# Layer 1 row loads moved behind other weights, and GpSimd's part of the stage reordered, in a two-layer graph kernel

## The chip, the cores and the metric

The kernel runs on one core of a Trainium2 chip. A core has TensorE for matrix products, VectorE and ScalarE for elementwise work, GpSimd (POOL in the profile) for elementwise work and for issuing transfers, and SyncE (SP), which only issues transfers. Sixteen DMA engines serve all queues. Times are device microseconds of the core, from separate executions; one more execution was taken under the profiler. The number to predict is the median time of the changed kernel.

## The reference, cut to what matters

Both layers work on 128 graphs of 64 nodes with 768 features, all in float32. Layer 0 is an attention whose weights come from the features themselves, with three linear maps (left, self, right). Layer 1 has twelve heads with maps q, k and v. Each is followed by a residual and a layer norm.

```python
x, adj: (128, 64, 768), (128, 64, 64)
# layer 0
u = softmax(h @ h.T / sqrt(768)) * adj;  attn = u / (sum(u) + 1e-10)
ctx = upper(attn) @ (h @ Wl.T + bl) + diag(attn) * (h @ Ws.T + bs) + lower(attn) @ (h @ Wr.T + br)
x = layernorm(x + relu(layernorm(ctx) * gamma + beta))
# layer 1
q, k, v = x @ Wq + bq, x @ Wk + bk, x @ Wv + bv        # 12 heads of 64
s = q @ k.T / 8 + beta * adj, masked to -9e15 where adj <= 0
x = layernorm(x + softmax(s) @ v)
```

## The kernel before, in words

The tokens are cut into 16 blocks of 512 (8 graphs). A block's tokens are four tiles `o` of 128 tokens by 768 features, and also a transposed form, with features on partitions, that feeds the products: `hT` for layer 0, `xT` for layer 1.

Products are done with fewer multiplications than the plain form, from sums of quarters (or sixths) of both factors. Weights in such summed forms lie ready in DRAM (`lr_d` for left and right together, `d_s` for self, `v_d`, `qk_d`) and are loaded anew for each block on SyncE's queue into rings of buffers: `wlr`, `ws`, `wv`, `wqk`. Sums of the token side are made by GpSimd: `combined` (L403) makes the operands of a layer 0 block and `second_level` (L467) their second sums `q`; `combined4` (L417, recorded as L420) makes the last operand, number 3; `fifteen` (L422) makes those of layer 1.

The loop over `n` (L1202) is a software pipeline: layer 1 of block `n` runs among layer 0 of block `m = n + 1` and the ends of block `p = n - 1`. Its stages for TensorE are, in order:

- left and right of block `m` together (`both_sides`, L761, matmuls L784), from `m = 3` on: seven products, each of seven inner ones, 49 steps in all. Nine `wlr` weights of the next product are loaded when the present one begins. The products come in the order 7, 1, 2, 6, 5, 4, 3. These 13 blocks are called deep here.
- self of block `m` (`self_part`, matmuls L520): seven products in two halves, 14 places, three `ws` weights each.
- `values` of block `n` (wv, L459), with the attention products of block `m` (L832) among them.
- `projected` of block `n`, twice (wqk, L459), for q and k.

The order of everything else is written out by hand with `at(hooks, place, f)`. `left` and `right` have 14 places each over the 49 steps; place `k` of both together comes ahead of step `49 k / 28`, with `right` counted from 14. `own` has 14 places in the self stage, `val` 15 in values, `qk[0]` and `qk[1]` 15 each. Short pieces are put into queues (`later`) and taken one by one in `step` after each product step. Every engine runs its instructions in the order in which they were recorded, so what stands in front in a queue holds up what stands behind.

The lines that the change touches:

- The output of layer 0, `o` of block `n`, is stored to DRAM as rows (`x1d`, L888, `stored`) by GpSimd and read back in another order (`sq`, L387, function `squares`) by SyncE: four loads of 384 KB, each into 32 partitions. VectorE turns `sq` into `xT` by six transposes (L396, `turned`). GpSimd's `fifteen` then makes the layer 1 sums. The buffer `sq` is a single one; after the sixth transpose ScalarE's queue loads the input rows of the next block into it, and VectorE makes `hT` from them in values.
- In a deep block the four loads stand at `right` 5 to 8, which is among the last steps of products 5 and 4; nine `wlr` of product 3 are recorded among them.
- `combined4` and the four stores stand at `left` 6; so they come between additions `o` (L1070) of the block before, which wait for VectorE's shares of attention (L1067).
- `out_dram` (L1107) is the output of the block before, four stores of 384 KB by GpSimd, which follow the norm by ScalarE (L1103) near the end of the left and right stage.

A transfer reports its landing on one of eight semaphores of the queue, taken in turn; SyncE waits, before it issues a transfer, until the transfer that had the same semaphore eight issues earlier has landed.

Of the kernel before, what the change touches and what calls it, by code (L numbers as in the profile page):

```python
# [17 lines left out]
P = 128  # L18
# [5 lines left out]
T = 4  # L24
# [28 lines left out]
DEEP = 3  # L53
# [16 lines left out]
def gnn_two_layers(ctx: ExitStack, tc, x, adj, wl, bl, ws, bs, wr, br, gamma, beta,  # L70
                   wq, bq, wk, bk, wv, bv, abeta, out):
    nc = tc.nc
# [51 lines left out]
    for half, sign in ((0, 1), (1, -1)):  # L124
        for g in range(2):
            nc.gpsimd.affine_select(
                out=side[half * L : (half + 1) * L, g, :], in_=side[half * L : (half + 1) * L, g, :],
# [4 lines left out]
    blocks = {}  # L132
# [44 lines left out]
    def freed():  # L177

        while first:
            first.popleft()[1]()  # L180
# [236 lines left out]
    def combined4(S, n=None):  # L417

        S[3] = sums[:, KC : KC + HC]
        last_sum[n] = nc.gpsimd.tensor_tensor(S[3], S[2], S[6], ALU.subtract)  # L420
# [391 lines left out]
    def context0(n):  # L812


        blk = blocks[n]
        o, dg = blk["x"], blk["dg"]
        by_act = n > 0
        if by_act:
            total, nm, var, std, rstd = (st.tile([P, T], F32, tag=f"c{k}", name=f"c{k}") for k in range(5))

        def unused():
            return l1s_p.tile([P, T * 6 * L], F32, tag="s", name="unused")[:, 0:D]

        banks = {}

        def multiplied(ts):
            freed()
            for t in ts:
                for h in range(2):
                    ps = banks[t, h] = ps_mm.tile([P, 512], F32, tag="mm", name="ps_ctx")  # L830
                    for g in range(2):
                        nc.tensor.matmul(ps[g * L : (g + 1) * L, 0:HALF], lhsT=blk["aT"][:, t, g * L : (g + 1) * L],  # L832
                                         rhs=blk["lr"][t][:, g, h * HALF : (h + 1) * HALF], start=True, stop=True)

        def part(t):
            if t % 2 == 0:
                multiplied((t, t + 1))
            for h in range(2):
                cols = slice(h * HALF, (h + 1) * HALF)
                nc.vector.scalar_tensor_tensor(o[t][:, cols], o[t][:, cols], dg[:, t : t + 1],  # L840
                                               banks.pop((t, h))[:, 0:HALF], ALU.mult, ALU.add)
            if by_act:
                nc.scalar.activation(unused(), o[t], AF.Identity, accum_out=total[:, t : t + 1])  # L843
            elif t == T - 1:
                rest(moments(key, o, 1e-12))

        key = ("o", n)

        def squares():
            nc.vector.tensor_scalar(nm, total, -1.0 / D, None, ALU.mult)  # L850
            for t in range(T):
                nc.scalar.activation(unused(), o[t], AF.Square, bias=nm[:, t : t + 1], accum_out=var[:, t : t + 1])

        def roots():
            nc.vector.tensor_scalar(std, var, 1.0 / D, 1e-12, ALU.mult, ALU.add)
            nc.scalar.activation(std, std, AF.Sqrt)

        def inverse():
            nc.vector.reciprocal(rstd, std)
            rest([(nm[:, t : t + 1], rstd[:, t : t + 1]) for t in range(T)])  # L860

        def affine(t, mean, rstd):
            nc.vector.scalar_tensor_tensor(o[t], o[t], mean, affine_of["gamma"], ALU.add if by_act else ALU.subtract,
                                           ALU.mult)

        def affine2(t, mean, rstd):
            nc.vector.scalar_tensor_tensor(o[t], o[t], rstd, affine_of["beta"], ALU.mult, ALU.add)

        def residual(t):
            nc.vector.scalar_tensor_tensor(o[t], o[t], 0.0, blk["xa"][t], ALU.max, ALU.add)  # L870

        squared = 0 < n < NBLK - 1
        blk["x_d"] = x_d = tc.dram_tile([NTOK, D], F32, name=f"x1d_{n}") if squared else None

        def lowered(mrs):
            for t, (mean, rstd) in enumerate(mrs):
                nc.vector.scalar_tensor_tensor(nm[:, t : t + 1], mean, -1.0, rstd, ALU.mult, ALU.mult)

        def norm(t, mean, rstd):
            if by_act and (n < NBLK - 1 or t % 2 == 0):  # L880
                nc.scalar.activation(o[t], o[t], AF.Identity, bias=nm[:, t : t + 1], scale=rstd)
            else:
                nc.vector.tensor_scalar(o[t], o[t], mean, rstd, ALU.subtract, ALU.mult)

        def stored():
            settle(key)
            for t in range(T):
                nc.gpsimd.dma_start(out=x_d[t * P : (t + 1) * P, :], in_=o[t])  # L888

        blk["stored"] = stored  # L890

        def rest(factors):
            for t, mr in enumerate(factors):
                fs = partial(affine, t, *mr), partial(affine2, t, *mr), partial(residual, t)
                later(key, *(fs if by_act else (fs[0], lambda fs=fs: (fs[1](), fs[2]()))))
            mrs = moments(key, o, 1e-5)
            fs = [partial(norm, t, *mr) for t, mr in enumerate(mrs)]
            later(key, *((tiny(partial(lowered, mrs)), *(f if n == NBLK - 1 and t % 2 else act(f) for t, f in enumerate(fs))) if by_act else
                         (lambda: (fs[0](), fs[1]()), lambda: (fs[2](), fs[3]()))))

        return [partial(part, t) for t in range(T)], (squares, roots, inverse)
# [300 lines left out]
    for n in range(NBLK):  # L1202
        m, p = n + 1, n - 1
        left, right, own, val = {}, {}, {}, {}
        qk = [{}, {}]

        def at(hooks, place, f, *args):
            hooks.setdefault(place, []).append(partial(f, *args))
# [24 lines left out]
        if not last:  # L1233
            if n > 0:
                if m + 1 < NBLK:
                    at(left, 4, edges, m + 1)
                at(*((left, 11) if m < DEEP else (right, 13)), sides, m)
                sq1 = {}

                def begin1():  # L1240
                    blocks[n]["sq1"], sq1["fs"] = squares(blocks[n]["x_d"], nc.sync)


                when, place = right, 5 if m >= DEEP else 10
                at(when, place, begin1)
                fetch = {}

                def begin2():
                    fetch["fs"] = loads(m)

                at(val, 3, begin2)
                for t in range(T):
                    at(val, 3 + t, lambda t=t: fetch["fs"][t]())
                for a in range(P // Q):
                    at(when, place + a, lambda a=a: sq1["fs"][a]())
                at(own, 0, settle, ("f", p))

                def turn1():
                    blocks[n]["xT"] = turned(("t1", n), blocks[n]["sq1"], f"xT_{n}")
                    later(("m", n), *mask(n), queue=urgent)  # L1260

                at(own, 3, turn1)

                def sums1():
                    settle(("t1", n))
                    blocks[n]["S"] = fifteen(blocks[n]["xT"], False)

                at(own, 11, sums1)
                at(val, 0, lambda: fifteenth(blocks[n]["S"]))
                at(left, 6, lambda: combined4(blocks[m]["S"]))  # L1270
                if n > 1:
                    for k in range(T):
                        at(left, 1 + k, begun, ("o", n), T - 1 - k)
                at(*((left, 6) if n > 1 else (right, 1)), blocks[n]["stored"])
                if m + 1 < NBLK:
                    sq = {}

                    def begin():
                        blocks[m + 1]["sq"], sq["fs"] = squares(x_b[m + 1])

                    at(own, 11, begin)
                    for a in range(P // Q):
                        at(own if a < 3 else val, 11 + a if a < 3 else 0, lambda a=a: sq["fs"][a]())
                if m == DEEP:
                    settle("d")
                if m < DEEP:
                    side_part(m, "l", None, left)
                    side_part(m, "r", None, right)
                    at(own, 0, lambda: nc.vector.tensor_tensor(bias_lr[:, :, HALF:D], bias_lr[:, :, HALF:D],
                                                               bias_lr[:, :, 0:HALF], ALU.subtract))  # L1290
                else:
                    for t, f in enumerate(both_sides(m, {**left, **{2 * len(ORDER) + k: f for k, f in right.items()}})):
                        at(own, 1 + t, f)
                self_part(m, None, own)
# [33 lines left out]
    n = NBLK - 1  # L1328
# [127 lines left out]
```

## Time and profile before

| what | us |
|---|---|
| median of 3 runs (lowest, highest) | 2916.44 (2909.95, 2923.62) |
| profiled execution | 2916.36 |
| its span, first to last instruction | 2914.3 |
| TensorE busy | 2807.8 |
| VectorE busy | 1950.4 |
| ScalarE busy | 1101.7 |
| GpSimd busy | 945.0 |
| granted TensorE clock, mean of the span | 0.991 |

A row of the timeline has start and length in microseconds, the engine (PE is TensorE, DVE VectorE, ACT ScalarE, POOL GpSimd, SPq SyncE's queue), the line, the operation, what it writes and reads, and in brackets how long the engine stood idle before it and what ended that. A row of the window view has busy time and count for each of PE, weight loads, DVE, ACT and POOL, then the granted clock, the share of the DMA engines' time in use, and GB/s. Clock and shares are fractions of one.

### The profile page before, as it was taken

To read this page: it belongs to the slowest core of one execution; us is meant where nothing else is said; L and a number is where in the kernel's file an instruction comes from. 1 tells how busy PE (TensorE), PEld (TensorE's weight loads), DVE (VectorE), ACT (ScalarE), POOL (GpSimd) and SP (SyncE) were. 2 spreads that over 40 slices of the span, in tenths; PEclk is the share of its full clock that TensorE was granted. 3 is DMA by queue.
4 is the path that set the end of the run, shared out by engine and by line. 5 is a ranking of instruction groups with operands and counts; after the bars stand their busy time and mean duration, and the time that the engine had idled before them with its cause. 6 is when DMAs were issued, how large, how long until landed. Compare 5 with 4: busy or idle time off the path is not lost.

```text
span 2914.3 us, 49295 instructions
## 1 busy us (share of the span) xinstructions
PE 2807.8 (96%) x17962; PEld 2019.9 (69%) x17962; DVE 1950.4 (67%) x3399; ACT 1101.7 (38%) x1907; POOL 945.0 (32%) x1231
## 2 busy tenths in 40 slices
PE   9999999999999999999998999999999999999997
PEld 5558677585776858668585775857758577685786
DVE  6787777575675766667676675766757567575655
ACT  0003324344343442535334343443434424344254
POOL 3234233514134151522615125141341414315121
PEclk9999999999999999999999999999999999999998
DMA  8788695948669486684957759586594866848542
GB/s 316 217 278 267 187 289 179 263 132 256 190 191 255 135 269 177 209 234 144 276 153 225 216 155 275 135 268 189 186 246 126 264 187 196 250 135 254 166 123 91
DMA packets 398493, 604.85 MB, mean 208 GB/s; under 512 B 49296, under 2 KB 282256, under 8 KB 398256
## 3 DMA queue, kind: packets, MB, share of 16 engines
q1 hardware_dynamic: 349520, 506.73, 59.3%
q0 software_dynamic: 17456, 72.96, 6.6%
q10 hardware_dynamic: 31280, 22.03, 3.7%
q8 instruction: 145, 2.38, 0.3%
q14 instruction: 92, 0.75, 0.1%
HBM read 530.00 MB, written 78.45 MB: 209 GB/s over the span
## 4 chain that ended last, share of the span: by engine, by line
PE 85%; DMA 7%; DVE 4%; issue 2%; POOL 1%; SPq 1%; ACT 1%; DVEq 0%; POOLq 0%; ACTq 0%
PE ps_X L459 25%; PE ps_Y L459 17%; PE ps_X L520 10%; PE ps_Y L784 10%; PE ps_X L784 8%; PE ps_Y L520 7%; DMA wlr<-lr_d 4%; PE ps_ctx L832 3%; PE sc L996 2%; PE u L663 2%; PE ps_y L1059 2%; DMA h_q<-in_L_gnn_Wq_dram 0%; POOL o L1070 0%; ACT eT L1029 0%; DMA h_v<-in_L_gnn_Wv_dram 0%
## 5 line engine op out<-in xcount | busy, mean ns | idle before, releaser
L408 POOL TENSOR_TENSOR sums<-hT 128x768 f32<-128x768 f32 x16 | 28.9, 1808 | 851.9 <-PE ps_X L459 841.2
L1029 ACT ACTIVATE eT<-s 32x384 f32<-32x384 f32 x512 | 266.6, 521 | 31.9 <-DVE s L1012 25.5
L1070 POOL TENSOR_TENSOR o<-o,share 128x192 f32<-128x192 f32 x240 | 134.7, 593 | 410.8 <-DVE share L1067 391.5
L574 DVE TENSOR_TENSOR lr<-ps_Y,u_deep 128x384 f32<-128x384 f32 x273 | 151.6, 555 | 140.2 <-PE ps_Y L784 123.9
L459 PE MATMUL ps_X<-xT,wqk 128*128 128x256 f32 x1024 | 236.0, 381 | 3.0 <-DMA wqk<-qk_d 2.0
L843 ACT ACTIVATE unused<-o 128x768 f32<-128x768 f32 x60 | 50.6, 843 | 476.4 <-DMA sq<-in_x_dram 227.5
L459 PEld LDWEIGHTS ps_X<-xT,wqk 128*128 128x128 f32 x1024 | 195.5, 191 | 30.7 <-DVE w_deep L362 2.4
L784 PE MATMUL ps_Y<-wlr,q 128*128 128x384 f32 x546 | 208.6, 491 | 0.0
L972 ACT ACTIVATE qk<-ps_X,bq 128x256 f32<-128x256 f32 x128 | 60.6, 473 | 388.8 <-PE ps_X L459 388.5
L975 DVE TENSOR_TENSOR qk<-qk,ps_X 128x512 f32<-128x512 f32 x160 | 109.8, 686 | 137.1 <-PE ps_X L459 74.7
L520 PE MATMUL ps_X<-ws,hT 128*128 128x384 f32 x540 | 179.8, 487 | 3.0 <-DVE u L551 3.0
L459 PE MATMUL ps_Y<-more,wqk 128*128 128x256 f32 x768 | 181.4, 379 | 0.0
L459 PE MATMUL ps_X<-sums,wqk 128*128 128x256 f32 x768 | 180.3, 381 | 0.5 <-issue 0.5
L784 PE MATMUL ps_X<-wlr,q 128*128 128x384 f32 x364 | 151.3, 497 | 19.5 <-issue 17.6
L459 PEld LDWEIGHTS ps_Y<-more,wqk 128*128 128x128 f32 x768 | 145.9, 190 | 19.8
L459 PEld LDWEIGHTS ps_X<-sums,wqk 128*128 128x128 f32 x768 | 144.6, 190 | 20.9 <-issue 0.9
L520 PEld LDWEIGHTS ps_X<-ws,hT 128*128 128x128 f32 x540 | 102.2, 190 | 74.8 <-DVE u L551 3.9
L975 DVE TENSOR_TENSOR qk<-qk,ps_Y 128x512 f32<-128x512 f32 x160 | 108.2, 677 | 67.7 <-PE ps_Y L459 65.1
L574 DVE TENSOR_TENSOR u_deep<-ps_X,lr 128x384 f32<-128x384 f32 x195 | 107.7, 553 | 66.7 <-PE ps_X L784 61.3
L784 PEld LDWEIGHTS ps_Y<-wlr,q 128*128 128x128 f32 x546 | 101.5, 190 | 67.3
L437 POOL TENSOR_TENSOR more<-xT 128x512 f32<-128x512 f32 x32 | 43.1, 1347 | 281.3 <-DVE xT L396 173.4
L784 PE MATMUL ps_X<-wlr,sums 128*128 128x384 f32 x234 | 93.7, 510 | 38.6 <-DMA wlr<-lr_d 35.8
(269 smaller groups left out, 6258.1 us busy)
## 6 DMA issues: line engine op xcount, KB each, us to landing
wlr<-lr_d SPq DMA_DIRECT2D x819, 192.0 KB, 4.1
wqk<-qk_d SPq DMA_DIRECT2D x480, 256.0 KB, 2.6
wv<-v_d SPq DMA_DIRECT2D x240, 256.0 KB, 6.2
ws<-d_s SPq DMA_DIRECT2D x180, 192.0 KB, 4.4
ws<-in_L_gnn_W_self_dram SPq DMA_DIRECT2D x135, 192.0 KB, 6.3
xa<-in_x_dram SPq DMA_DIRECT2D x64, 384.0 KB, 5.8
out_dram<-o POOLq DMA_DIRECT2D x60, 384.0 KB, 6.5
sq<-in_x_dram ACTq DMA_DIRECT2D x56, 384.0 KB, 10.8
```

The lines of the kernel that those rows point to most:

```text
L459: nc.tensor.matmul(ps[:, h, :], lhsT=a, rhs=b, start=start and h == 0 and k == 0, stop=k == len(fs[h]) - 1, skip_group_check=True)
L520: nc.tensor.matmul(ps, lhsT=a, rhs=b, start=(c == 0 and i in (1, 2, 5)), stop=(c == len(fs) - 1), skip_group_check=True)
L574: nc.vector.tensor_tensor(dst, view(ps), add, ALU.add)
L663: nc.tensor.matmul(u[g * L : (g + 1) * L, t, :], lhsT=xT[:, c, tok], rhs=xT[:, c, tok], start=(c == 0), stop=(c == KC - 1))
L784: nc.tensor.matmul(ps, lhsT=a, rhs=b, start=(k == 0 and j in (1, 2, 5)), stop=(k == len(fs) - 1), skip_group_check=True)
L832: nc.tensor.matmul(ps[g * L : (g + 1) * L, 0:HALF], lhsT=blk["aT"][:, t, g * L : (g + 1) * L], rhs=blk["lr"][t][:, g, h * HALF : (h + 1) * ...
L972: nc.scalar.activation(dst[:, h], ps[:, h, :], AF.Identity, bias=bias["qk"[h]][:, c : c + 1], scale=float(sign))
L975: nc.vector.tensor_tensor(dst, dst, ps, ALU.add if sign > 0 else ALU.subtract)
L996: nc.tensor.matmul(sc[t // 2, r][g * L : (g + 1) * L, t % 2, c, :], lhsT=q[rows, c, tok], rhs=k[rows, c, tok], start=True, stop=True)
L1029: nc.scalar.activation(e[to[0], :, to[1]], pairs[rows, :, cols], AF.Exp, scale=1.0 / SCALE)
L1059: nc.tensor.matmul(y[h, r][cols, t, c, :], lhsT=eT[rows, 2 * h + t, c, cols], rhs=by_parity[rows, 2 * h + t, 2 * c + m, g, :], start=True, ...
L1070: nc.gpsimd.tensor_tensor(res, res, share[:, t], ALU.add)
```

## The change

The four loads of layer 1 rows move from `right` 5 to 8 to `right` 12 and 13 and `own` 0 and 1 (before block 3 they stood at `right` 10 to 13). As SyncE's queue stands in a deep block, the first three now come behind the nine `wlr` of the last product and ahead of the first three `ws`, and the fourth behind these three. The transposes of `xT` begin at `own` 4, not `own` 3, and the mask's three VectorE instructions, queued behind them, follow.

On GpSimd `combined4` moves from `left` 6 to `left` 1: its subtraction is recorded right after the last of `combined` and ahead of the first additions `o`. The row stores, four together before, are recorded one at a time at `left` 5 to 8: the first directly behind the subtraction, the second after four additions `o`, the last two after four more. In block 1 they stay at `right` 1. TensorE's and ScalarE's instructions keep their order.

```diff
-        def stored():
+        def stored(t):
             settle(key)
-            for t in range(T):
-                nc.gpsimd.dma_start(out=x_d[t * P : (t + 1) * P, :], in_=o[t])
+            nc.gpsimd.dma_start(out=x_d[t * P : (t + 1) * P, :], in_=o[t])
...
-                when, place = right, 5 if m >= DEEP else 10
-                at(when, place, begin1)
+                at(right, 12, begin1)
...
                 for a in range(P // Q):
-                    at(when, place + a, lambda a=a: sq1["fs"][a]())
+                    at(*((right, 12 + a) if a < 2 else (own, a - 2)), lambda a=a: sq1["fs"][a]())
...
-                at(own, 3, turn1)
+                at(own, 4, turn1)
...
-                at(left, 6, lambda: combined4(blocks[m]["S"]))
+                at(left, 1, lambda: combined4(blocks[m]["S"]))
...
-                at(*((left, 6) if n > 1 else (right, 1)), blocks[n]["stored"])
+                for t in range(T):
+                    at(*((left, 5 + t) if n > 1 else (right, 1)), blocks[n]["stored"], t)
```

## The prediction

> **What bounds the kernel now.** I read the page first: busy time, slices and the chain.
>
> ```profile
> span 2914.3 us, 49295 instructions
> PE 2807.8 (96%) x17962; PEld 2019.9 (69%) x17962; DVE 1950.4 (67%) x3399; ACT 1101.7 (38%) x1907; POOL 945.0 (32%) x1231
> PE 85%; DMA 7%; DVE 4%; issue 2%; POOL 1%; SPq 1%; ACT 1%; DVEq 0%; POOLq 0%; ACTq 0%
> ```
>
> TensorE is busy for 2807.8 of 2914.3 us, so everything that an order of transfers can save lies in the other 106.5 us and in matmuls that run slowly. The chain puts 7% on DMA. To find where, I read TensorE's timeline for its idle marks. Apart from the start and the end they repeat in each of the 13 deep blocks. One block:
>
> ```profile
> start us, us, engine line op out<-in xcount [idle before <-releaser]
> 1210.84 0.88 PE L784 MATMUL ps_X<-wlr,q 128*128 128x384 f32 x2 [1.47 <-issue]
> ...
> 1237.70 1.08 PE L784 MATMUL ps_X<-wlr,sums 128*128 128x384 f32 x2 [2.59 <-DMA wlr<-lr_d]
> 1238.75 2.90 PE L784 MATMUL ps_Y<-wlr,sums 128*128 128x384 f32 x4
> ...
> 1247.53 1.56 PE L784 MATMUL ps_X<-wlr,sums 128*128 128x384 f32 x4 [0.21 <-DVE u_deep L574]
> 1250.21 4.03 PE L520 MATMUL ps_X<-ws,hT 128*128 128x384 f32 x12
> ```
>
> The second mark is the one that this change aims at: the first matmul on the last of the seven products (operand 3) waits for its weights. The next row shows a second cost: four matmuls in 2.90 us, where such a group takes 1.45. SyncE's timeline of the same block says why the weights are late: three row loads stand ahead of them in its queue.
>
> ```profile
> 1225.85 1.38 SPq L387 DMA_DIRECT2D sq<-x1d  x3
> 1227.33 10.86 SPq L775 DMA_DIRECT2D wlr<-lr_d  x9
> 1238.63 0.32 SPq L387 DMA_DIRECT2D sq<-x1d  x1
> 1239.12 4.51 SPq L545 DMA_DIRECT2D ws<-in_L_gnn_W_self_dram  x6
> ```
>
> Nine weight loads, 0.5 us each to issue, are spread over 10.86 us. Landings of these nine, then the median of all 819 from the page:
>
> ```profile
> DMA to landing us min/median/max: 5.8/9.5/10.6
> wlr<-lr_d SPq DMA_DIRECT2D x819, 192.0 KB, 4.1
> ```
>
> **What the stall costs.** From the matmul after the 1.47 mark to the matmul after the 0.21 mark the 13 blocks take 34.0, 39.0, 34.0, 33.6, 36.7, 33.6, 40.1, 33.6, 35.9, 38.1, 38.6, 34.0 and 38.3 us. Taking the stall off four of the short ones leaves 32.3 to 32.6; I use 32.3. The excess over it adds up to 49.7 us: the most that moving the row loads can give back.
>
> **The change, part by part.**
>
> *Row loads (SyncE).* In each deep block three of four loads leave their place ahead of the last nine wlr and go behind them, ahead of the first ws; the fourth goes behind three ws. No transfer is added or removed, so the same bytes pass later. That removes the 49.7 us. What is late next is ws, the self stage's weights, and SyncE's queue holds them behind the rows. I keep a ledger of DMA service with durations from the trace: successive row loads land 2.0 us apart, successive 192 KB weights 0.52 us apart, and the four out stores of 384 KB issued by GpSimd put out their first packets about 3.3 us after issue.
>
> Blocks are of two kinds. In "early" ones (seven) the nine wlr find free buffers. In "late" ones (six, every second) a later one waits for a buffer. SyncE's longest wait in such a block (in all, times, longest):
>
> ```profile
> SPq L775 <- PE ps_X L784: 3.5, 1, 3.5
> ```
>
> and the window view a little later in it (after the busy times: granted clock, DMA share, GB/s):
>
> ```profile
> 1425.00:1430.00 5.00, 5.00 (x17) 2.92 (x16) 1.63 (x3) 3.60 (x5) 0.00 (x0) 1.00 1.02 405
> ```
>
> The DMA engines are full there already (a share of 1.02).
>
> Late block (the rows at 1404): today the row loads fill the 3.5 us hole. After the change it stays empty: the second wlr is still issued at 1409.5, so the last of the nine lands at 1409.5 + 4.1 + 7 x 0.5 = 1417, the three row loads at 1419, 1421, 1423. Then three ws need 1.56 us. But the out stores (issued at 1420.2) start to move at 1423.5. The packet records of 1424 to 1428 show 214 store packets of 6144 B at 235 ns and 202 weight packets of 1536 B at 66 ns: nearly one for one, so weights get about a fifth of the time. The stores need 3.8 us by themselves and occupy 4.7. Weights get 1.0 in it, and the third ws lands at about 1428.7. TensorE, without the 0.93 stall, would come to ws at 1424.5, and to the third 0.65 later: 3.5 us late. The next three ws with the fourth row load (3.6 us of service) land at 1432, about when they are needed.
>
> Early block (rows at 1225): nine wlr land by 1236, rows by 1242, three ws by 1243.6; TensorE wants them at 1250.21 - 4.4 = 1245.8. No wait. The fourth row load and three more ws then meet the stores (moving from 1243 to 1248) and are up to 1 us late. I take 1.0.
>
> *First rule against the change.* The Trainium skill, "DMA: Bandwidth & Descriptors", section "Queues, rings and completion order": each DMA engine takes turns between queue rows, a packet at a time. The measured turns above are for 1536-byte packets; a row load is 768-byte packets (about 62 ns), for which no row shows a contest with stores. By the rule its share is 62/(62+234), again a fifth, and the fourth load in a late block is starved as charged. With an equal split of time the backlog at 1423.5 would clear in 3.1 us, by 1426.6, and a late block would pay 1.5 instead of 3.5. I take the rule's end; the other is in the range.
>
> *Clock.* Three rows of the window view, one after the 2.59 us stall, two around one of 3.64 us:
>
> ```profile
> 1237.60:1241.50 3.90, 3.80 (x7) 1.87 (x8) 0.56 (x1) 0.00 (x0) 3.74 (x6) 0.58 1.03 301
> 1946.50:1950.00 3.50, 0.00 (x0) 0.00 (x0) 1.76 (x3) 1.24 (x2) 3.42 (x4) 1.00 1.11 258
> 1950.00:1954.00 4.00, 3.88 (x12) 2.38 (x13) 1.81 (x5) 0.65 (x1) 3.14 (x6) 1.00 1.09 323
> ```
>
> After an idle 2.59 us the clock is 0.58 for 3.9 us; after 3.64 us idle it is not lowered at all. Of the seven stalls above 2.5 us six were followed by slow matmuls, which cost about 1.8 us each. The Trainium skill ("TensorE: Matmul & The Clock Gate", Part 1) sets the loss at an idle window of about 3.4 us, free-running. By the rule alone the six late blocks at 3.5 us would pay 6 x 1.8 = 10.8, or nothing if the stalls come out at 3.0; by the row, 6/7 of it. I take 1.5 a late block, 9 in all.
>
> *GpSimd's last sum first (L420, 1.81 us), row stores spread (four of 0.54 us).* Priced at nothing. The sum moves to just after L414, where GpSimd has a 22 us hole:
>
> ```profile
> 1177.41 1.82 POOL L414 TENSOR_TENSOR sums<-sums,hT 128x768 f32<-128x768 f32 x1
> 1201.56 1.14 POOL L1070 TENSOR_TENSOR o<-o,share 128x192 f32<-128x192 f32 x2 [22.33 <-DVE share L1067]
> 1205.80 1.81 POOL L420 TENSOR_TENSOR sums<-hT,sums 128x768 f32<-128x768 f32 x1
> 1207.56 2.17 POOL L888 DMA_DIRECT2D x1d<-o  x4
> ```
>
> It waits there for TensorE's last read of that buffer (about 1184) and still ends 15 us before the o rows. The first store follows it, and needs ScalarE's norm, done by 1190. The last two stores pass behind four o rows, issued at about 1209.5 instead of 1209; the row loads wait for all four, which land by 1217, and are issued from 1233 on: 16 us of cover. Gone, it would cost its excess one for one. Nothing waited for operand 3's sum 27 us early, so no gain either.
>
> *Transposes of xT one place later (own 3 to 4), mask after them (VectorE).* The sixth ends about 2 us later, 1272 for 1270. Two things queue on it. GpSimd's layer 1 sums end 1276.9 for the product that needs them at 1287.1: 10 us of cover. ScalarE's four loads of the next block's rows reuse the buffer; the last lands 2.1 to 5.2 us before VectorE's first hT transpose, so 2 us later just fits. If not, VectorE waits with the v evictions behind it, up to 2 us a block.
>
> *VectorE behind the stall.* TensorE's pause let VectorE catch up with its evictions at operand 3; without it the 0.21 mark may double: 13 x 0.25 = 3.
>
> *The sum.* -49.7, + 7 x 1.0 early, + 6 x (3.5 + 1.5) late, + 3 VectorE, and + 6 because blocks of one kind differ by several us today and the ledger takes the smooth one (0.5 a block): -3.7 us. The profiled execution took 2916.36 us (its span 2914.3 and 2 around it), the median shown is 2916.44: 2913.
>
> **Rivals.**
> 1. *The wait is gone.* Late blocks behave as early ones: 13 x 1.0 + 3 - 49.7 = -34, 2882; with nothing paid at all, 2867. For it: early blocks show slack at ws (the first lands 3.7 us before its use today). Against it: the full DMA share until 1430 in the late block.
> 2. *Slower: the stores overtake the rows everywhere.* Place: the self stage's first three ws. It decides when the third row load lands after the out stores' first packets, as in late blocks; the early block has about 1 us to spare (1242 to 1243). Then all 13 pay 5.0: 65 + 3 - 49.7 = +18, and with the scatter and some hT waits 2934 to 2945.
> 3. *It does not do what it says:* the nine wlr are slow from buffers and not from the rows. The late block's 3.5 us hole is for it; the early block, where issues stop until rows land (1232.7, 1234.7, 1237.3), is against. Time as before, 2916, inside the forecast.
>
> **How the numbers follow.** About 0.5% (14.6 us) is what a measurement of this kernel tells from no change. Forecast with rival 3: 0.46, own range 2902 to 2931. Rival 1: 0.30, below 2902. Rival 2: 0.24, above 2931. The 8-in-10 range cuts a tenth at each end: 2880 to 2940, so faster 0.30, same 0.46, slower 0.24.
>
> **What would show it.** Right: no mark at wlr,sums from DMA in deep blocks; a DMA mark at ps_X<-ws or ps_Y<-ws in every second block, some 3 us, with clock below 1 behind it; ws issued ahead of the stores landing in over 9 us; TensorE busy time unchanged within 10 us. Wrong: no ws marks (rival 1), ws marks in all blocks (rival 2), marks at v evictions, or an o or sums row waiting on the moved GpSimd work.

## The result, and the profile after

The changed kernel takes 2923.8 us (median of 12 runs, 2915.0 to 2928.5), the kernel before 2920.0 over 12 runs measured beside it (2910.0 to 2923.6). The ratio is 1.0016, 95% interval 1.0004 to 1.0029: slower by 0.16%, and within the 0.5% that the prediction took for no change. The forecast of 2913 was 11 us too low, and its sign was wrong.

The profiled execution took 2923.47 us, with a span of 2921.7; before, the span was 2914.3. From the page after, the lines that answer to the first three shown of before:

```profile
span 2921.7 us, 49293 instructions
PE 2806.6 (96%) x17962; PEld 2014.2 (69%) x17962; DVE 1962.7 (67%) x3399; ACT 1102.2 (38%) x1907; POOL 947.4 (32%) x1231
PE 76%; POOL 9%; DMA 8%; DVE 4%; issue 1%; ACT 1%; SPq 1%; DVEq 0%; POOLq 0%; ACTq 0%
```

TensorE's busy time hardly differs (2806.6 for 2807.8). In the chain GpSimd has 9%, where it had 1%, and TensorE has 76%, where it had 85%. The waits of TensorE, by what ended them, say what that is (us in total, times, longest). First the kernel before:

```profile
PE ps_X L784 <- DMA wlr<-lr_d: 36.6, 14, 5.3
PE ps_X L784 <- issue: 17.6, 12, 1.5
...
PE ps_Y L784 <- DMA wlr<-lr_d: 0.4, 1, 0.4
...
PE ps_X L784 <- POOL q L473: 0.2, 1, 0.2
```

And after:

```profile
PE ps_X L784 <- POOL q L473: 36.3, 26, 1.7
PE ps_Y L520 <- DMA ws<-in_L_gnn_W_self_dram: 21.8, 15, 2.7
...
PE ps_X L520 <- DMA ws<-in_L_gnn_W_self_dram: 3.2, 7, 1.5
...
PE ps_X L784 <- DMA wlr<-lr_d: 2.3, 2, 2.1
```

Three things have happened. The wait at `wlr` has gone, as the change intended: 36.6 us became 2.3. A wait at `ws` of 25.0 us has come, as the prediction said. And a wait for GpSimd's sums `q` has come, of which the prediction said nothing. Of its 26 marks 13 are the 1.47 mark, which mostly had no name before ("issue") and has kept its length; only the name is new. The other 13, 17 us in all, are new. Here is one, in TensorE's timeline of the block that the prediction showed:

```profile
1217.13 0.88 PE L784 MATMUL ps_X<-wlr,q 128*128 128x384 f32 x2 [1.48 <-POOL q L473]
...
1244.47 1.45 PE L784 MATMUL ps_Y<-wlr,q 128*128 128x384 f32 x4
1247.26 0.91 PE L784 MATMUL ps_X<-wlr,q 128*128 128x384 f32 x2 [1.33 <-POOL q L473]
...
1250.76 1.56 PE L784 MATMUL ps_X<-wlr,sums 128*128 128x384 f32 x4 [0.21 <-DVE u_deep L574]
1252.15 1.45 PE L784 MATMUL ps_Y<-wlr,q 128*128 128x384 f32 x4
1253.44 2.74 PE L520 MATMUL ps_X<-ws,hT 128*128 128x384 f32 x8
```

The 2.59 mark at `wlr,sums` is no longer there. Some steps later, inside product 3, TensorE waits for the small sums `q` of that product's operand. GpSimd's timeline of the same stretch:

```profile
1225.72 1.14 POOL L1069 TENSOR_TENSOR o<-o,share 128x192 f32<-128x192 f32 x2 [7.69 <-DVE share L1066]
...
1243.23 1.00 POOL L589 TENSOR_TENSOR lr<-lr,lr 128x384 f32<-128x384 f32 x1
1244.19 1.00 POOL L588 TENSOR_TENSOR lr<-lr,bias_lr 128x384 f32<-128x384 f32 x1
1245.26 1.00 POOL L589 TENSOR_TENSOR lr<-lr,lr 128x384 f32<-128x384 f32 x1
1246.21 0.46 POOL L472 TENSOR_TENSOR q<-sums 128x128 f32<-128x128 f32 x1
1246.75 0.46 POOL L473 TENSOR_TENSOR q<-q,sums 128x128 f32<-128x128 f32 x1
```

From 1225.72 on GpSimd has no idle mark: 21.5 us of additions, and `q` is ready at 1247.2. The same row stood in the kernel before:

```profile
1219.43 1.14 POOL L1070 TENSOR_TENSOR o<-o,share 128x192 f32<-128x192 f32 x2 [5.42 <-DVE share L1067]
...
1238.93 0.99 POOL L589 TENSOR_TENSOR lr<-lr,lr 128x384 f32<-128x384 f32 x1
1239.88 0.45 POOL L472 TENSOR_TENSOR q<-sums 128x128 f32<-128x128 f32 x1
1240.42 0.45 POOL L473 TENSOR_TENSOR q<-q,sums 128x128 f32<-128x128 f32 x1
```

In both, the row begins, when VectorE's share is there, 8.6 us behind TensorE's 1.47 mark (1219.43 - 1210.84 and 1225.72 - 1217.13), and `q` is ready 30.0 us behind it. TensorE by itself needs 28.8 us for that way (1217.13 to 1245.93). So 1.33 us were always missing; in the kernel before, TensorE came later, because it had waited for weights. The stage can't be shorter than GpSimd's row lets it be; this least time is called GpSimd's floor here. One block of before shows it by name: the single wait of 0.2 us for `q` in the list above belongs to the block that begins at 1365.76, where the weights were late by only 0.93 us.

**The stages of the 13 deep blocks.** "Left and right" is the time from the first wlr matmul of a block to its first ws matmul, "self" from there to its first wv matmul, both from TensorE's timeline. Values took 31.76 us in each of these blocks in both kernels, q and k 56.70 (57.7 in one). Sums over the 13 blocks are from one profiled execution each, which need not be near the median: it took 2914.2 us in rows_only, 2905.3 in spread_q3, 2922.2 in q3_early2 and 2938.4 in twice_before. The medians are of all runs, and each ratio is against runs of the kernel before on the same chip.

| kernel | median us | ratio (95%) | left and right, sum | shortest | self, sum |
|---|---|---|---|---|---|
| before | 2920.0 | 1 | 809.5 | 59.65 | 352.2 |
| after | 2923.8 | 1.0016 (1.0004 to 1.0029) | 782.8 | 59.65 | 384.9 |
| rows_only | 2921.5 | 1.0008 (0.9990 to 1.0025) | 782.6 | 59.61 | 376.8 |
| gpsimd_only | 2923.6 | 1.0009 (0.9999 to 1.0019) | 812.3 | 59.61 | 352.2 |
| no_rows | 2889.6 | 0.9892 (0.9862 to 0.9922) | 782.3 | 59.62 | 352.2 |
| no_out | 2892.2 | 0.9901 (0.9886 to 0.9916) | 780.3 | 59.61 | 357.4 |
| q3_early2 | 2930.3 | 1.0030 (1.0013 to 1.0047) | 767.7 | 58.05 | 395.8 |
| spread | 2890.4 | 0.9900 (0.9883 to 0.9917) | 781.3 | 59.61 | 353.0 |
| spread_only | 2890.3 | 0.9898 (0.9882 to 0.9913) | 777.6 | 59.59 | 357.1 |
| spread_q3 | 2895.3 | 0.9905 (0.9886 to 0.9924) | 769.0 | 58.04 | 372.6 |
| spread4 | 2891.0 | 0.9899 (0.9873 to 0.9925) | 781.0 | 59.61 | 352.2 |
| spread4_q3 | 2876.5 | 0.9850 (0.9828 to 0.9871) | 764.4 | 58.05 | 352.2 |
| twice_before | 2932.5 | 1.0037 (1.0023 to 1.0050) | 829.2 | 61.64 | 352.2 |
| twice_spread | 2931.8 | 1.0042 (1.0029 to 1.0055) | 824.4 | 61.67 | 352.2 |

Self takes 27.09 us when nothing is waited for (13 x 27.09 = 352.2). Left and right is never shorter than 59.6 us, in any kernel that leaves GpSimd's late row as it is. The difference after - before is -26.7 in left and right and +32.7 in self; the start, q and k, and the end bring the other 1.3 of the 7.4 us between the spans.

### The profile page after: what moved, and what is told of

Same layout as the page of the kernel before. It is cut to its first block, busy times and chain, and to the rows that moved or that the text cites. A ratio compares the mean times of both kernels' runs of the same rounds, so it can differ in the third digit from the quotient of the medians.

```text
span 2921.7 us, 49293 instructions
## 1 busy us (share of the span) xinstructions
PE 2806.6 (96%) x17962; PEld 2014.2 (69%) x17962; DVE 1962.7 (67%) x3399; ACT 1102.2 (38%) x1907; POOL 947.4 (32%) x1231
## 4 chain that ended last, share of the span: by engine, by line
PE 76%; POOL 9%; DMA 8%; DVE 4%; issue 1%; ACT 1%; SPq 1%; DVEq 0%; POOLq 0%; ACTq 0%
PE ps_X L459 24%; PE ps_Y L459 16%; PE ps_X L520 9%; PE ps_Y L520 8%; PE ps_Y L784 6%; PE ps_X L784 5%; DMA ws<-in_L_gnn_W_self_dram 5%; POOL o L1069 3%; PE ps_ctx L832 2%; PE u L663 2%; PE sc L995 2%; PE ps_y L1058 2%; POOL lr L589 1%; POOL lr L588 1%; POOL q L473 1%
## 5 line engine op out<-in xcount | busy, mean ns | idle before, releaser
L784 PEld LDWEIGHTS ps_X<-wlr,q 128*128 128x128 f32 x364 | 63.7, 189 | 103.5 <-POOL q L473 51.9
```

The lines of the kernel that those rows point to most:

```text
L784: nc.tensor.matmul(ps, lhsT=a, rhs=b, start=(k == 0 and j in (1, 2, 5)), stop=(k == len(fs) - 1), skip_group_check=True)
```

## The experiments

### Which part of the change, and whose floor

rows_only is the kernel before with the row loads and the transposes moved, and nothing on GpSimd:

```diff
-                when, place = right, 5 if m >= DEEP else 10
-                at(when, place, begin1)
+                at(right, 12, begin1)
...
-                    at(when, place + a, lambda a=a: sq1["fs"][a]())
+                    at(*((right, 12 + a) if a < 2 else (own, a - 2)), lambda a=a: sq1["fs"][a]())
...
-                at(own, 3, turn1)
+                at(own, 4, turn1)
```

> The kernel before with the row loads and the transposes moved as in the change, and GpSimd's queue as it was. Theory G (GpSimd has its own floor: from the 1.47 mark in the third product, GpSimd needs 30 us for its additions up to the operand sums of the last product, with the moved sum or without): 13 marks of about 1.33 us at ps_X<-wlr,q behind GpSimd, left and right stage 59.65 us in most blocks, time within 3 us of the changed kernel (2921 to 2927). Rival M (the moved sum and the spread row stores make GpSimd late): these marks are gone, 13 x 1.3 = 17 us less than the changed kernel, about 2907.

gpsimd_only has the other part alone (`combined4` at `left` 1, one store each at `left` 5 to 8).

> The kernel before with only GpSimd's part of the change (last sum first, row stores spread). Theory G: as the kernel before, within 3 us of 2920; 13 marks at wlr,sums of some 36 us in all stay, no new marks at q. Rival M: GpSimd is late by itself, part of the wlr marks turns into marks at q, and blocks whose stall is short become longer than 59.65 us: 5 to 15 us slower than before.

Theory G holds and rival M falls. rows_only has the 13 marks of 1.3 us with GpSimd's queue in its old order, the waits of TensorE in it being:

```profile
PE ps_X L784 <- POOL q L473: 16.6, 13, 1.3
PE ps_X L784 <- issue: 14.9, 11, 1.5
PE ps_Y L520 <- DMA ws<-in_L_gnn_W_self_dram: 13.8, 9, 2.6
```

Here the 1.47 marks are mostly called "issue" again, and the 13 of 1.3 us stand alone. gpsimd_only keeps the wlr wait (35.9 us). Its median is 4 us above that of before, where theory G had 3 at most, but the interval of the ratio (0.9999 to 1.0019) takes in 1: what the moved sum and the spread stores cost can't be told from zero.

### Was the floor there before?

In q3_early2 the four sums `q` of operand 3 are made right behind the operand, into memory that nobody reads at that time (for a third buffer of their own there is no room):

```diff
         last_sum[n] = nc.gpsimd.tensor_tensor(S[3], S[2], S[6], ALU.subtract)
+        if "deep" in S:
+            S["deep"][3] = second_level(S[3], home[:, 0:5, 0:P])
...
```

> The changed kernel with the four small sums q of operand 3 (2.1 us) made right after the operand itself, early in the stage, in the part of the last block's xT that nobody reads any more, and so taken out of GpSimd's late row of additions. Theory G: the 13 marks of 1.33 us at ps_X<-wlr,q go, left and right stage 58.3 us where nothing else waits; but the self weights land no sooner, so in the 11 blocks with a mark at ws the 1.33 us come back there: between -17 (nothing comes back) and -3 us (only two blocks gain), I expect about 2916. Rival (the wait is not for GpSimd's sums, the name is only the last event): no change, 2924.

The 13 marks went: left and right falls to 58.05 us at its shortest and by 15.1 us in all. But self grows by 10.9, and the median is 6.5 us above that of the changed kernel where 8 less was expected. The mechanism was right, its worth was not: in the profiled execution most of what TensorE gained was waited for at ws. That the median rose on top of it was not explained.

In slow_before and slow_spread (below for the latter's base) operand 3's sum was computed a second time just ahead of `q`, with the same values.

```diff
         def sums(i):
+            if i == 3:
+                combined4(blk["S"])
             return blk["S"]["deep"].get(i) or second_level(blk["S"][i])
```

> The kernel before with operand 3's sum (L420, 1.81 us, same values) computed a second time on GpSimd just ahead of its sums q, so that GpSimd is 1.81 us later there. Theory G (the wait at wlr lies over GpSimd's floor of 59.65 us): no left and right stage is shorter than 61.46 us; the blocks that stood at 59.65 to 60.1 rise to it, those of 61.9 us and more stay; with the stage times of the profile before that is 9 us in all, 2929. Rival (GpSimd has time to spare in the kernel before): no change. Rival (GpSimd sets every block): 13 x 1.81 = 24 us.

> The same second sum in the kernel with one row load at a time, where no weight is waited for. Theory G: every block pays it, 11 to 13 x 1.81 = 20 to 24 us more than without, 2910 to 2914. Rival (GpSimd has time to spare): 2890.

Both missed: 2986.2 (ratio 1.0227, 1.0208 to 1.0246) and 2988.5 (1.0237, 1.0220 to 1.0254). The edit was put in the wrong place. The second sum writes operand 3 itself, and the first step of product 3 reads that, well ahead of the step that reads `q`. From TensorE's waits in slow_before:

```profile
PE ps_X L786 <- POOL sums L420: 66.1, 10, 6.6
PE ps_X L786 <- DMA sq<-x1d: 19.8, 3, 6.6
```

These 13 waits of 6.6 us are at `wlr,sums` (for three of them another event is named). So the runs measured another dependency: a sum this late is paid for in full. They say nothing on the floor, and the test was made again with something that only the step in question reads. twice_before and twice_spread make `q` of operand 3 twice, into the same buffer:

```diff
...
         def sums(i):
+            if i == 3:
+                q = s2_p.tile([P, 5, P], F32, name="q", tag="q")
+                second_level(blk["S"][i], q)
+                return second_level(blk["S"][i], q)
             return blk["S"]["deep"].get(i) or second_level(blk["S"][i])
```

> The kernel before with the four sums q of operand 3 made twice on GpSimd, one after the other (the same values, 2.1 us more, and nothing but the sixth-place step of product 3 reads them). Theory G (GpSimd's floor of 59.65 us lay under the wait at wlr): no left and right stage is shorter than 61.75 us; with the stage times of the profile before, the blocks below that rise by 11 us in all and those of 61.9 us and more stay: about 2931. Rival (GpSimd had 2 us to spare in the kernel before): 2920. Rival (GpSimd sets every block there): 13 x 2.1 = 27 us, 2947.

> The same in the kernel with one row load at a time, where hardly a weight is waited for. Theory G: nearly every block pays the 2.1 us, the two that stand above the floor less: 11 x 2.1 to 13 x 2.1, 23 to 27 us, 2913 to 2917. Rival (time to spare): 2890.

twice_before came as theory G had it: 2932.5, 11 us above the 2921.1 beside it, and its shortest left and right stages are 61.64 us for 61.75 expected. In five blocks TensorE now waits for `q` by name:

```profile
PE ps_X L789 <- POOL q L474: 8.6, 5, 2.2
```

The profiled execution was the slowest of the five (2938.4), and its left and right stages are 19.7 us longer than before, not 11; the shortest stages and the median bear the argument. A change that delays GpSimd by 2.1 us and nothing else lengthens the short blocks of the kernel before. The floor was there, under the wait for weights.

twice_spread pays more than expected, 41 us over spread and not 23 to 27. Left and right grew by 43.1, of which 13 x 2.05 = 26.7 is the floor (61.67 for 59.62). Most of the rest is clock. Two rows of its window view, each just behind an idle of 3.35 us (after the busy times: granted clock, DMA share, GB/s):

```profile
1070.00:1074.00 4.00, 3.77 (x14) 2.30 (x15) 1.62 (x4) 0.00 (x0) 3.15 (x6) 1.00 1.10 253
1424.50:1428.50 4.00, 4.00 (x7) 2.18 (x8) 0.56 (x1) 0.00 (x0) 3.11 (x6) 0.50 1.11 220
```

Half as many matmuls in the second. Eight blocks have such slow matmuls, which cost some 16 us by the spacing of their starts. Why one idle has this effect and not the other is told at the end.

### Rows, stores and the self weights

no_rows leaves out layer 1's row loads in deep blocks and lets the transposes read what `sq` holds; layer 1 then computes on other data.

> The changed kernel without layer 1's row loads in the deep blocks (xT is made from what sq still holds, so layer 1 computes on other data; everything else is as it was). Theory W (the rows' 8 us of transfer ahead of ws push ws into the out stores): no marks at ws, self stage 27.1 us in all 13 blocks, 33 us less than the changed kernel, about 2891; left and right stays at 59.65, so not more than that. Rival (the out stores by themselves, or ws buffers, hold ws up): marks at ws of 15 us or more stay, about 2905 or above.

no_out leaves out the out stores of blocks 1 to 13; these rows of the output aren't written.

```diff
-            for t in ts:
+            for t in ts if not 0 < n < NBLK - 2 else ():
```

> The changed kernel without the out stores of blocks 1 to 13 (so these rows of the output are not written; everything is computed). Theory W2 (rows and stores together: the rows push ws to where the stores take four fifths of the transfer time): the marks at ws shrink from 25 us to under 8 and the slow matmuls behind them go, self stage under 28 us in all blocks, time about 2896. Rival W1 (the rows alone are enough, the stores only pass by): marks at ws stay above 17 us, time above 2912.

Both are nearly as theory W had it: without rows self is 27.09 us in all blocks, and without stores it loses 27.5 of the 32.7 us, though three blocks stay at 28.1 to 28.2 where under 28 was expected. Stores alone cost nothing at ws and rows alone 5.2 us; most of the wait needs both. A late block of the changed kernel shows it, in SyncE's timeline and then in TensorE's:

```profile
1406.59 10.52 SPq L775 DMA_DIRECT2D wlr<-lr_d  x10
1417.33 1.38 SPq L387 DMA_DIRECT2D sq<-x1d  x3
1418.76 2.67 SPq L545 DMA_DIRECT2D ws<-in_L_gnn_W_self_dram  x3
1421.47 0.55 SPq L387 DMA_DIRECT2D sq<-x1d  x1
1422.12 4.68 SPq L545 DMA_DIRECT2D ws<-in_L_gnn_W_self_dram  x3
```

```profile
1428.92 0.88 PE L520 MATMUL ps_X<-ws,hT 128*128 128x384 f32 x2
1430.19 3.77 PE L520 MATMUL ps_X<-ws,hT 128*128 128x384 f32 x10 [0.39 <-DMA ws<-in_L_gnn_W_self_dram]
1436.34 3.90 PE L520 MATMUL ps_Y<-ws,hT 128*128 128x384 f32 x6 [2.38 <-DMA ws<-in_L_gnn_W_self_dram]
```

The 2.38 us are not at the first three ws but at the three behind the fourth row load, which was issued at 1421.5, landed at 1435.8 and shared its way with the out stores (issued from 1423.4).

### One row at a time

In spread the four loads stand singly: ahead of the nine weights of product 4, ahead of those of product 3, behind these, and behind the first three ws.

```diff
-                at(right, 12, begin1)
+                at(right, 2 if m >= DEEP else 12, begin1)
...
-                    at(*((right, 12 + a) if a < 2 else (own, a - 2)), lambda a=a: sq1["fs"][a]())
+                    at(*(((right, 2), (right, 7), (right, 12), (own, 1)) if m >= DEEP else ((right, 12), (right, 13), (own, 0), (own, 1)))[a], lambda a=a: sq1["fs"][a]())
```

> The changed kernel with the row loads one at a time: one ahead of the nine weights of product 4 (right 2), one ahead of those of product 3 (right 7), one behind these (right 12), one behind the first three ws (own 1). Theory S (slack: with three rows of 2.0 us ahead product 3 waited 2.6 us in an early block, so a group of nine has about 3.4 us to spare and one row fits; ws get 4 us back, more than their longest mark of 2.7): no marks at wlr, few at ws, left and right at GpSimd's floor of 59.65 us, self 27.1: about 2893, near the kernel without rows. Rival (the transfers are full, and the rows' 8 us are paid wherever they stand): 2912 or more, with marks at wlr or ws of 20 us in all.

Theory S holds: 2890.4, 1.0% faster than the kernel before (interval 0.9883 to 0.9917) and within a microsecond of no_rows, where no row is loaded at all. 13 x 8 us of transfers are hidden, with no more than one of them ahead of any group of weights. spread_only, the same on the kernel before, without GpSimd's part, gives the same:

> The kernel before with the row loads one at a time and nothing of GpSimd's part. If the moved sum and the spread row stores neither give nor cost anything: as one at a time with them, 2888 to 2894. If they are what keeps GpSimd at its floor: above 2897.

It took 2890.3: GpSimd's part isn't needed for this gain. spread4 puts each row load one group earlier (`left` 12, `right` 2, 7 and 12) and the four stores together behind the moved sum.

> As one row load at a time, but one place earlier each (ahead of the weights of products 5, 4 and 3 and ahead of ws), with the four row stores together right behind the moved sum, so that they land in time. Theory S: ws land about 2 us earlier than with one at a time, the left and right stage stays at GpSimd's 59.65 us, self 27.1: 2884 to 2892, as one at a time within its scatter. Rival (product 5 has no slack for a row): marks at wlr of 10 us or more, above 2897.

2891.0, as expected. Then both with `q` of operand 3 made early:

> The row loads one at a time as in the kernel before this, and the sums q of operand 3 made early. Theory G and S together: the floor of the left and right stage falls by 1.33 us and nothing takes it back: 13 x 1.33 = 17 us less than one at a time alone, about 2876. Rival (behind GpSimd's sums the weights or VectorE's evictions stand at nearly the same time): under 6 us less.

> The kernel before this with the sums q of operand 3 made early. Theory (GpSimd's floor and then the landing of ws, each shown alone: with q early the left and right stage fell to 58.06 us, and 13 to 20 us came back at ws): with ws 2 us earlier nearly nothing comes back, 13 x 1.6 = 21 us less than the kernel before this, about 2868. Rival (the transfers are full from the start of the stage to the middle of self, so TensorE can't run ahead of them): self stays above 28 us in most blocks, above 2882.

spread_q3 missed. Left and right lost 12.3 us and self got 19.6 longer, with 13.4 us of marks at ws, in an execution that was its slowest, and five blocks wait for product 3's weights again (0.8 to 2.0 us); by the medians too it is no faster than spread. spread4_q3 took 2876.5, 1.5% faster than the kernel before: left and right loses 16.6 and self stays at 352.2. In its shortest blocks the idle marks, by TensorE's timeline, are two:

```profile
1379.84 0.88 PE L787 MATMUL ps_X<-wlr,q 128*128 128x384 f32 x2 [1.47 <-POOL q L478]
...
1411.84 1.56 PE L787 MATMUL ps_X<-wlr,sums 128*128 128x384 f32 x4 [0.21 <-DVE u_deep L577]
```

So two limits lay close behind the wait that the change removed, GpSimd's `q` and the landing of ws. Taking away one brings out the other (q3_early2, spread_q3, or spread, which stays at GpSimd's floor); with both away the gain is kept. It was 14.5 us less than spread4 for 21 expected: with the floor lowered, five blocks wait for the weights of product 3 again, 0.3 to 1.0 us each.

## Why the prediction was wrong, by its own steps

| term, us | forecast | measured, profile to profile |
|---|---|---|
| wait at operand 3, between the two marks | -49.7 | -32.6 |
| left and right ahead of the 1.47 mark | 0 | +3.5 |
| ws waits with their clock | +37 | +35.2 |
| VectorE | +3 | 0 |
| scatter; start, q and k, and end | +6 | +1.3 |
| sum | -3.7 | +7.4 |

**What the stall costs: the step that failed.** "Taking the stall off four of the short ones leaves 32.3 to 32.6; I use 32.3." This takes TensorE's own time for the time of the stage, and puts at nothing what GpSimd needs for `q`. After, the same stretch takes 33.6 us in all 13 blocks, 437.0 in all for 469.5 before: 32.6 us were given back, and 17.1 of the 49.7 weren't there to be had. The list of block times had the sign of it: three blocks at 33.6, though their stalls were 0.93, 1.36 and 1.00 (0.65 and 0.35). Blocks with unequal stalls and one time point to a floor that something else sets. The prediction even asked the right question, what an engine does when TensorE no longer pauses, and asked it of VectorE alone (its mark stayed at 0.21), not of GpSimd, whose 21 us without an idle mark were in the timeline of before.

**Late next.** The price of the ws waits came out well. By blocks, counting the wait ahead of the first ws matmul: six late blocks 25.6 (forecast 30), seven early ones 9.6 (forecast 7). The place was off by one group. The third ws of the block at 1405 was forecast for 1428.7, which is 1431.9 in the time of after (this block begins 3.2 us later there), and landed at 1431.1. But TensorE came to ws 1.2 us later than forecast, 0.9 of it because of GpSimd and 0.3 for the first ws itself, and found the third nearly there; the starved fourth row load then held up the next three, which landed at 1436.3 to 1437.4 for a forecast of 1435.2. Not every second block but 11 of 13 have a mark. The clock was to cost 9 us; slow matmuls followed two of the ws waits (2.20 and 2.38 us) and cost some 3.5 in all.

**The first rule** (packets in turn) fits. In the microseconds 1077 to 1080 of after, in a late block, the records have 56, 54, 53 and 53 store packets against 68, 56, 60 and 53 of rows and weights: nearly one for one, also where rows took part (a packet is one record of the trace here). A row packet took 36 ns in these, not the 62 that the prediction charged. **The second**, an idle window that runs free, fits in part: the traces show such windows, but an idle need not fill one (see the end).

**GpSimd's part at nothing:** right, as far as can be told (rows_only, gpsimd_only, spread_only). The cover of the sum is worth having: made once more just ahead of its use, it cost some 65 us. **Transposes later:** right, values took 31.76 us in each of the 13 blocks, the same as in the kernel before. **+3.5 ahead of the mark:** not foreseen. 3.0 of it is one block, whose first weights came 2.07 us late; that this comes from the change was not shown.

**Rivals.** Rival 2 (rows overtaken everywhere) had the better sign, but not its place: early blocks paid 1.4 us each, not 5. That the sum came within 11 us, with 17 us wrong in one term, is luck: 9 us of allowances (VectorE and scatter) were hardly needed and made up for part of the gain that wasn't there.

## What to carry to other kernels

Before a wait is counted as a saving, follow each other engine that the same stage needs, from its last idle mark to the instruction that TensorE reads, and ask when TensorE would come without the wait: the saving ends at the next engine's time. Equal block times at unequal stalls are a sign of such a floor. A group of transfers that is in the way as a whole can be free one by one: three rows ahead of nine weights cost up to 5.3 us, one cost nothing while GpSimd's floor lay over it, and up to 2.0 where that floor was lowered (spread_q3). The slack can be estimated from the stall itself (three rows of 2.0 us and a wait of 2.6 leave about 3.4).

## What the hardware showed unexpectedly

Idle time of one length had two outcomes. In twice_spread the longest idles of product 3 in the first five deep blocks, 3.04, 3.24, 3.14, 3.35 and 2.25 us, left the clock alone; in each of the eight blocks after them one of 1.94 to 3.36 us was followed by a lowered clock. The clock records of the traces show what decides. Within a run every stretch of lowered clock begins a whole number of steps of 3.413 us from every other, as if on a fixed grid. Here are the two idles of 3.35 us again, in windows cut along the grid of that run:

```profile
1064.74:1068.15 3.41, 1.92 (x6) 0.77 (x5) 2.17 (x5) 2.20 (x3) 3.25 (x6) 1.00 1.06 202
1068.15:1071.57 3.42, 1.55 (x5) 1.03 (x6) 0.56 (x1) 1.58 (x2) 3.34 (x8) 1.00 1.11 235
1419.73:1423.14 3.41, 1.38 (x5) 0.49 (x3) 1.67 (x3) 2.74 (x3) 3.25 (x6) 1.00 1.03 205
1423.14:1426.55 3.41, 2.08 (x4) 1.18 (x5) 0.40 (x1) 1.05 (x2) 3.33 (x8) 0.50 1.12 226
```

The first idle is split into 1.5 and 1.9 us, and the clock stays full. The second leaves 2.0 us in one step (1.38 busy of 3.41), and the next step runs at half the clock. In the 16 traces, from 350 us on, 96 of some 11,760 steps at full clock were followed by a lowered one: all those with more than 2.0 us of idle, none with less than 1.79, and some of those between. The prediction's two rows come out of this too: its 2.59 us lay in one step, its 3.64 were split into 1.74 and 1.90. So do the 2.38 us (in one step, lowered) and the 2.72 (1.17 and 1.55, not lowered) of the changed kernel. So it is not the length of an idle that counts but how much of it falls into one step, and where the grid lies differs from run to run.

Row packets of 768 B went at 250 a microsecond, 68 to 72 ns each, when rows had the engines nearly to themselves (after, 1067 to 1070), about the time of a weight packet of twice the size (65 to 70 ns). So 192 KB of rows took a microsecond of all engines there. In turn with stores, at 1077, they took 36 ns; but so did half of them at 1066, at the start of the same loads, with few other packets beside them. What makes the difference is not shown.

A name in the wait list can change without its cause: the 1.47 mark is "issue" before, `q` L473 after, and `q` L475 in spread4, 1.47 us long in nearly every block of each. What ends it was not tested.
